# Moving a softmax's reciprocals one beat later and its products two beats later in a fused graph-attention kernel

## The chip, the cores and the metric

The kernel runs on one core of a Trainium2 chip. The time is that of one execution on the device, in microseconds; the median of several runs counts.

## The reference, cut to what matters

Two layers over x of 8 x 2048 x 256 (float32) and a 0/1 adjacency matrix of 2048 x 2048. Layer 0 is an attention of four heads whose softmax runs over each chunk of 256 keys separately; the eight chunks' results are added:

```python
scores = jnp.einsum('bhnd,bhjcd->bhnjc', q, kc) / jnp.sqrt(Dh)
scores = jnp.clip(scores, -10.0, 10.0)
scores = jnp.where(mask == 0, -10.0, scores)
attn = jax.nn.softmax(scores, axis=-1)          # over the 256 keys of one chunk
ctx = jnp.einsum('bhnjc,bhjcd->bhnd', attn, vc)
out = layernorm(ctx @ Wo.T + bo + x) * gamma + beta
h = layernorm(x + out)
```

Layer 1 is a graph attention with one head on h:

```python
Wh = h @ W;  e = leaky_relu(s_i[:, None] + s_j[None, :])    # s_i = Wh @ a1, s_j = Wh @ a2
e = where(adj > 0 or diagonal, e, -inf)
out = layernorm(h + elu(softmax(e) @ Wh))
```

## The kernel before, in words

The kernel writes the order of every engine's work out by hand. For each of 8 batches (b) and 4 blocks of 512 queries (ib) it walks over 8 chunks (j) of 256 keys, J counting all 256 chunks. A chunk takes two **beats** of 128 keys each (`half` 0 and 1, here even and odd), so that there are 512 beats with attention (`2 * total`), and then beats of the tail that hold only layer 1 and the ends of blocks.

In one beat `begin_beat` starts steps of layer 1; then PE computes the scores of the beat (`sc`, line 775, into one of only two PSUM buffers of pool `ps_s`), DVE clips and masks them in place (line 785), ACT exponentiates them (`e`, line 788), and `middle_of_beat` masks layer 1's weights. Then PE multiplies the exponentials of the chunk before (`prev`) with the values and with ones (line 801): in the even beat part 2, the sums over the keys, and part 0, half of the values; in the odd beat part 1, the other half. ACT copies the values' products into `un` and the sums into `ds`. `end_beat` follows.

A chunk's softmax is divided only behind the product with the values. The sums go by a DMA into a narrow tile `dc` of 128 x 16, DVE takes the reciprocals (`inverse`, line 823), a DMA stores them to DRAM (`rd`), another loads them back spread over the partitions (`r`, function `spread`), and `scaled` multiplies `un` by `r` on DVE (line 836, or 834 for the first chunk) and adds the product into `ctxT` on POOL (line 837). These three functions are put on an agenda by the beat at which they are to be issued: `inverse` and `spread` for the end of the same beat, `scaled` for two beats later, so that in an even beat the product of the chunk before stands ahead of the reciprocals of this one.

`end_beat` issues in this order: layer 1's matmuls for the steps whose weights are ready (`product`), one step of every generator in `ahead` and `fins`, and then the agenda. The generators are

- `prelude`, which prepares layer 1 of a batch: Wh, and for every row the largest neighbour (`half_max`, line 412, on DVE, with loads `fb` on the SP queue), once all four blocks of the batch have left layer 0 (`fin_near`). `last_prelude` does so for the last batch in the tail.
- `fin`, the end of a layer-0 block: load x, add biases on POOL, wait, the output projection `po` of ctxT (line 331), two normalisations, h to DRAM, the transpose of h.
- `fin1`, the end of a layer-1 block: load `hr` (h) from DRAM, divide, `ex` = exp(hx - 1) on ACT, minimum and maximum on DVE (line 572), add `hr` on POOL (line 573), normalise, store the output.

A layer-1 step takes 128 keys: `low` on ACT, `leaky` on DVE (line 615), `edges` on DVE (line 620), the exponential on ACT, an addition into `acc` on POOL, and the matmuls `us` on PE (line 643, or 658 for the last batch). Up to 1.5 steps a beat are started, 1.1 while the last batch is in layer 0, and 1 in the tail. Every DMA is issued by the one SP queue, in the order of the program; an entry that waits holds up all behind it.

## Time and profile before

| | |
|---|---|
| median of 3 runs | 4439.85 us (4435.65 to 4445.19) |
| profiled execution | 4440.12 us, span of its instructions 4438.3 us |
| mean granted clock of TensorE | 0.975 |
| first and last score matmul of the attention | 36.7 and 4133 us |
| busy: PE, DVE, ACT, POOL | 92%, 77%, 59%, 40% |
| bytes moved | 432.93 MB, mean 98 GB/s |

Times in the profile are microseconds from the span's start, taken in one execution. PE is TensorE's matmuls, PEld its weight loads, DVE VectorE, ACT ScalarE, POOL GpSimd, SP the engine that issues the DMAs. `out<-in` names what an instruction writes and reads, `L785` the line of the kernel. A row of the waits reads: who waited, for whom, us in total, times, the longest. A row of the stages reads: from:to, length, busy us of PE, PEld, DVE, ACT and POOL with their instructions, granted clock, share of DMA time, GB/s. A row of the timeline reads: start, length, engine, line, operation, operands, how many, and in brackets the engine's idle time ahead of it with what ended it.

### The profile page before, as it was taken

To read this page: it belongs to the slowest core of one execution; us is meant where nothing else is said; L and a number is where in the kernel's file an instruction comes from. 1 tells how busy PE (TensorE), PEld (TensorE's weight loads), DVE (VectorE), ACT (ScalarE), POOL (GpSimd) and SP (SyncE) were. 2 spreads that over 40 slices of the span, in tenths; PEclk is the share of its full clock that TensorE was granted. 3 is DMA by queue.
4 is the path that set the end of the run, shared out by engine and by line. 5 is a ranking of instruction groups with operands and counts; after the bars stand their busy time and mean duration, and the time that the engine had idled before them with its cause. 6 is when DMAs were issued, how large, how long until landed. Compare 5 with 4: busy or idle time off the path is not lost. (4 is left out here: it accounts for less than half of the span.)

```text
span 4438.3 us, 61328 instructions
## 1 busy us (share of the span) xinstructions
PE 4076.7 (92%) x23053; PEld 1913.9 (43%) x23053; DVE 3412.6 (77%) x4530; ACT 2604.1 (59%) x3878; POOL 1782.7 (40%) x906
## 2 busy tenths in 40 slices
PE   7888999999899999999989999999989999899767
PEld 3222334444344443445434453444534445344455
DVE  4776468985799758996599966898569975898786
ACT  4666456665556655666556655566555665566455
POOL 0222224553255523554334543455325543355521
PEclk9999999999999999999999999999999999999889
DMA  4555333322322323223333223332332232332321
GB/s 145 165 161 154 93 104 102 96 89 82 102 84 90 100 67 113 86 79 95 93 92 101 82 75 106 97 105 74 90 105 83 92 96 75 109 94 78 117 79 53
DMA packets 266601, 432.93 MB, mean 98 GB/s; under 512 B 85952, under 2 KB 121024, under 8 KB 265408
## 3 DMA queue, kind: packets, MB, share of 16 engines
q1 hardware_dynamic: 266304, 429.01, 31.5%
q8 instruction: 181, 2.97, 0.3%
q14 instruction: 116, 0.95, 0.1%
HBM read 357.96 MB, written 68.88 MB: 96 GB/s over the span
## 5 line engine op out<-in xcount | busy, mean ns | idle before, releaser
L788 ACT ACTIVATE e<-sc 128x1024 f32<-128x1024 f32 x1024 | 1037.3, 1022 | 1144.9 <-DVE sc L785 1100.5
L785 DVE SCALAR_TENSOR_TENSOR sc<-sc,mk 128x1024 f32<-128x1024 f32 x1024 | 1205.5, 1221 | 519.6 <-PE sc L775 287.1
L775 PE MATMUL sc<-qT,kT 64*128 64x512 f32 x4096 | 1063.6, 633 | 108.6 <-ACT e L788 105.9
L837 POOL TENSOR_TENSOR ctxT<-ctxT,un 128x1024 f32<-128x1024 f32 x224 | 564.9, 2522 | 1173.6 <-DVE un L836 1068.1
L801 PE MATMUL u<-e,v 128*32 128x512 f32 x8192 | 982.5, 597 | 0.0
L643 PE MATMUL us<-wh,w 128*128 128x256 f32 x3584 | 875.9, 393 | 74.3 <-ACT w L624 56.6
L643 PEld LDWEIGHTS us<-wh,w 128*128 128x128 f32 x3584 | 663.9, 192 | 416.6 <-ACT w L624 110.6
L633 POOL TENSOR_TENSOR acc<-acc,w 128x512 f32<-128x512 f32 x392 | 607.8, 1551 | 528.6 <-ACT w L624 512.7
L775 PEld LDWEIGHTS sc<-qT,kT 64*128 64x128 f32 x4096 | 347.5, 189 | 631.3 <-ACT e L788 310.8
L615 DVE SCALAR_TENSOR_TENSOR w<-ab,sj,w 128x512 f32<-128x512 f32 x512 | 587.6, 1168 | 15.4 <-ACT w L611 15.3
L801 PEld LDWEIGHTS u<-e,v 128*32 128x32 f32 x8192 | 240.3, 110 | 660.2 <-issue 539.6
L620 DVE TENSOR_TENSOR w<-w,mk 128x512 f32<-128x512 f32 x512 | 467.8, 934 | 42.9 <-DMA mk<-mask 40.0
L801 PE MATMUL u<-e,ones 128*32 128x512 f32 x4096 | 497.8, 604 | 0.0
L412 DVE CUSTOM_DVE_ANT_0 fb<-sj_row,fb 128x1024 bf16<-128x1024 f32 x240 | 383.8, 1608 | 2.4 <-DMA fb<-far 2.4
L611 ACT ACTIVATE w<-ab,sj 128x512 f32<-128x512 f32 x512 | 353.7, 716 | 18.0 <-PE us L658 11.9
L624 ACT ACTIVATE w<-w 128x512 f32<-128x512 f32 x512 | 310.5, 631 | 66.3 <-DVE w L620 64.9
L836 DVE TENSOR_TENSOR un<-un,r 128x1024 f32<-128x1024 f32 x224 | 278.8, 1244 | 88.2 <-DMA r<-rd 72.7
L809 ACT COPY un<-u 128x512 f32<-128x512 f32 x512 | 300.6, 587 | 54.8 <-PE u L801 52.9
L801 PEld LDWEIGHTS u<-e,ones 128*32 128x32 f32 x4096 | 107.7, 110 | 357.3 <-issue 315.7
L823 DVE RECIPROCAL dc<-dc 128x16 f32<-128x16 f32 x256 | 64.1, 250 | 180.3 <-DMA dc<-ds 155.2
L573 POOL TENSOR_TENSOR hx<-hx,hr 128x1024 f32<-128x1024 f32 x32 | 91.6, 2862 | 177.8 <-DVE hx L572 177.8
L658 PE MATMUL us<-wh,w 128*128 128x257 f32 x512 | 127.6, 412 | 28.8 <-ACT w L624 28.8
(100 smaller groups left out, 3163.1 us busy)
## 6 DMA issues: line engine op xcount, KB each, us to landing
r<-rd SPq DMA_DIRECT2D x256, 256.0 KB
mk<-mask SPq DMA_DIRECT2D x120, 512.0 KB
fb<-far SPq DMA_DIRECT2D x240, 256.0 KB
xT_k<-in_xT_dram SPq DMA_DIRECT2D x32, 512.0 KB
raw<-in_adjT_dram SPq DMA_DIRECT2D x32, 512.0 KB
xT_q<-in_xT_dram SPq DMA_DIRECT2D x32, 512.0 KB
rawf<-in_adj_dram SPq DMA_DIRECT2D x32, 512.0 KB
xT_v<-in_xT_dram SPq DMA_DIRECT2D x32, 512.0 KB
```

Of the source, the lines that this page charges most:

```text
L412: nc.vector.tensor_tensor_reduce(out=fb, in0=sj_row[:, ts(hf, HN)], in1=fb, scale=1.0, scalar=2 * FAR * 0.999, op0=ALU.add, op1=ALU.max, a ...
L611: nc.scalar.activation(self.w, k["ab"][:, 1, :], AF.Identity, bias=k["sj"][:, 1, c : c + 1])
L615: nc.vector.scalar_tensor_tensor(self.w, k["ab"][:, 0, :], k["sj"][:, 0, c : c + 1], self.w, ALU.add, ALU.max)
L620: nc.vector.tensor_tensor(self.w, self.w, self.k["mks"][self.c // HT][:, self.c % HT, :], ALU.min)
L624: nc.scalar.activation(self.w, self.w, AF.Exp)
L633: nc.gpsimd.tensor_add(k["acc"], k["acc"], self.w)
L643: nc.tensor.matmul(k["us"][:, t, :], self.w[:, ts(t, P)], k["wh"][:, c, 0:F], start=(first and t % 2 == 0), stop=last, skip_group_check=True,)
L775: nc.tensor.matmul(sc[:, h, :], kT[h * D : (h + 1) * D, hp, ts(c, P)], qT[h * D : (h + 1) * D, hp, :], start=True, stop=True,)
L785: nc.vector.scalar_tensor_tensor(scs[hp], scs[hp], -CLIP, cap, ALU.max, ALU.min)
L788: nc.scalar.activation(e, scs[hp], AF.Exp)
L801: nc.tensor.matmul(m[h * DH : (h + 1) * DH, :], prev["v"][:, pc, f0 : f0 + DH] if part < 2 else ones[:, 0:DH], prev["es"][2 * i + h // 2][ ...
L837: nc.gpsimd.tensor_add(p["ctxT"], p["ctxT"], p["un"])
```

## The change

- The agenda is issued at the start of `end_beat`, ahead of layer 1's matmuls and of the generators.
- While attention runs, `inverse` and `spread` are issued one beat later, and `scaled` two beats later (`lag`); for the last chunk they keep their beats.
- `fin` no longer counts beats: it waits until the product of the block's last chunk has been issued (`ctx_done`), and while attention runs until the beat behind that.
- `un` gets a third buffer. The space comes from `ds` (one buffer for two) and from `ex`, which now takes turns with `hr` in one buffer; the load of `hr` is therefore issued behind the minimum and maximum that read `ex`, and `fin1` has one beat more before the addition. The second half of `a_bc`, which had `ex`'s place at the start, has that of `y`.

```diff
-        t = one.tile([P, F], F32, tag=("hx", "ex")[n], name=f"a_bc{n}")
+        t = one.tile([P, F], F32, tag=("hx", "y")[n], name=f"a_bc{n}")
...
+    ctx_done = {}
...
         nc.gpsimd.tensor_add(xt, xt, bc_rows(beta_bc))
-        yield
-        yield
-        yield
+        while (b, ib) not in ctx_done or ctx_done[b, ib] == beat < 2 * total:
+            yield
...
     def fin1(b, ib, hx, acc):
-        hr = one.tile([P, TPB, F], F32, tag="hr", name=f"hr{b}_{ib}")
-        nc.sync.dma_start(out=hr, in_=h_d[b, ib])
         yield
...
-        ex = one.tile([P, TPB, F], F32, tag="ex", name=f"ex{b}_{ib}")
+        ex = one.tile([P, TPB, F], F32, tag="hr", name=f"ex{b}_{ib}")
         nc.scalar.activation(ex, hx, AF.Exp, bias=shifts[:, 2:3])
         yield
         nc.vector.scalar_tensor_tensor(hx, ex, 1.0, hx, ALU.min, ALU.max)
+        hr = one.tile([P, TPB, F], F32, tag="hr", name=f"hr{b}_{ib}")
+        nc.sync.dma_start(out=hr, in_=h_d[b, ib])
+        yield
         nc.gpsimd.tensor_add(hx, hx, hr)
...
     def end_beat():
         nonlocal weighted
+        for fn in agenda.pop(beat, []):
+            fn()
         for s in weighted:
             s.product()
         weighted = []
         for gens in (ahead, fins) if beat < 2 * total else (fins, ahead):
             for g in list(gens):
                 if next(g, g) is g:
                     gens.remove(g)
-        for fn in agenda.pop(beat, []):
-            fn()
...
-                    prev["un"] = two.tile([P, 2, IB], F32, tag="un", name=f"un{prev['name']}")
+                    prev["un"] = three.tile([P, 2, IB], F32, tag="un", name=f"un{prev['name']}")
...
-                        ds = two.tile([P, IB], F32, tag="ds", name=f"ds{prev['name']}")
+                        ds = one.tile([P, IB], F32, tag="ds", name=f"ds{prev['name']}")
...
+                            if p["j"] == NCH - 1:
+                                ctx_done[p["b"], p["ib"]] = beat
                             if p["j"] == NCH - 3:
                                 fins.append(fin(p["b"], p["ib"], p["ctxT"]))
-                        at(beat, inverse)
-                        at(beat, spread)
-                        at(beat + 2, scaled)
+                        lag = 1 if J < total else 0
+                        at(beat + lag, inverse)
+                        at(beat + lag, spread)
+                        at(beat + 2 + 2 * lag, scaled)
```

More of the change, by code (lines that the diff above doesn't have):

```diff
@@ L308, in bc_rows @@
         return v.unsqueeze(1).to_broadcast([P, TPB, F])
+    total = B * NIB * NCH
     h_d = dram.tile([B, NIB, P, TPB, F], F32, name="h_d")
@@ L584, in tile_adj_attention__then__gat @@
     states = [{"ab": {}} for _ in range(B)]
-    total = B * NIB * NCH
     def layer1():
```

## The prediction

> **What bounds the kernel now.** I read the page first, then the waits of PE, then busy time by stage, then the timeline around the moved instructions. The page's first part and four of its groups (after the bar: busy us and mean ns; then the idle time of that engine just ahead, and what ended it):
>
> ```profile
> PE 4076.7 (92%) x23053; PEld 1913.9 (43%) x23053; DVE 3412.6 (77%) x4530; ACT 2604.1 (59%) x3878; POOL 1782.7 (40%) x906
> ...
> L837 POOL TENSOR_TENSOR ctxT<-ctxT,un 128x1024 f32<-128x1024 f32 x224 | 564.9, 2522 | 1173.6 <-DVE un L836 1068.1
> ...
> L412 DVE CUSTOM_DVE_ANT_0 fb<-sj_row,fb 128x1024 bf16<-128x1024 f32 x240 | 383.8, 1608 | 2.4 <-DMA fb<-far 2.4
> ...
> L836 DVE TENSOR_TENSOR un<-un,r 128x1024 f32<-128x1024 f32 x224 | 278.8, 1244 | 88.2 <-DMA r<-rd 72.7
> ...
> L823 DVE RECIPROCAL dc<-dc 128x16 f32<-128x16 f32 x256 | 64.1, 250 | 180.3 <-DMA dc<-ds 155.2
> ```
>
> PE sets the time. The change can remove no PE work, only PE's idle time, and it aims at two DVE waits: 180 us ahead of the reciprocals and 88 us ahead of the products. Those 268 us are idle time of an engine that is 77% busy, so they are not yet time of the kernel. By stage (head with the masks, steady loop, tail without attention):
>
> ```profile
> 36.70:494.60 457.90, 383.21 (x2204) 127.97 (x2204) 301.54 (x422) 268.62 (x335) 106.44 (x46) 0.93 0.48 149
> 494.60:4141.50 3646.90, 3468.94 (x19991) 1615.29 (x19991) 2883.34 (x3736) 2175.15 (x3270) 1596.93 (x814) 0.99 0.30 91
> 4141.50:4438.30 296.80, 202.10 (x820) 161.54 (x818) 224.42 (x361) 148.77 (x260) 78.57 (x41) 0.86 0.24 81
> ```
>
> The first number after the comma is PE: 75 us idle in the first stretch, 178 in the second, 95 in the tail, which the change hardly touches. So what can be won lies in 253 us. PE's waits in those first two stretches:
>
> ```profile
> PE sc L775 <- ACT e L788: 105.9, 72, 6.9
> PE po L331 <- POOL ctxT L837: 23.3, 15, 5.1
> PE pq L252 <- ACT un L809: 23.0, 14, 4.6
> PE us L643 <- ACT w L624: 22.3, 33, 2.5
> ```
>
> The largest is the score matmul that waits for the exponential freeing its PSUM buffer: the exponential waits for the clip, and the clip for DVE. One place, in order of time:
>
> ```profile
> 1197.74 0.56 SPq L817 DMA_DIRECT2D dc<-ds  x1
> ...
> 1197.89 1.23 DVE L836 TENSOR_TENSOR un<-un,r 128x1024 f32<-128x1024 f32 x1 [1.23 <-DMA r<-rd]
> ...
> 1201.38 0.25 DVE L823 RECIPROCAL dc<-dc 128x16 f32<-128x16 f32 x1 [2.27 <-DMA dc<-ds]
> 1201.55 2.33 DVE L785 SCALAR_TENSOR_TENSOR sc<-sc,mk 128x1024 f32<-128x1024 f32 x2
> ...
> 1202.79 2.15 ACT L788 ACTIVATE e<-sc 128x1024 f32<-128x1024 f32 x2 [1.97 <-DVE sc L785]
> ...
> 1203.87 2.26 PE L775 MATMUL sc<-qT,kT 64*128 64x512 f32 x8 [1.18 <-ACT e L788]
> ```
>
> DVE is idle 2.27 us until the 8 KB of sums land, the clips behind it start that much late, and 1.18 us of it reach PE. A beat's slack eats the rest.
>
> **How much of the waits reaches PE.** I followed each of PE's waits of the two stretches back by releasers: the exponential, its clip, then DVE's unbroken run of work back to where DVE was last idle. Of 254 us, 99 lead to a wait for dc (63 at score matmuls, 20 at pq, 10 at pw, 6 elsewhere), 12 to a wait for r, 64 to y<-po (DVE waiting for the output projection), 18 to a mask load, and 61 to other places. Where PE's wait is longer than the cause, only the cause can go: the lesser of the two, summed over dc and r, is 94 us.
>
> **Part by part.** A beat of the first half ("even") issues both u products and the copy into ds; the other is "odd".
>
> *Reciprocals.* The reciprocal goes from the end of an even beat to the odd beat behind, after its clips. The 0.56 us issue and the landing (together 3.6 us in the excerpt, from 1197.74 to 1201.38) then have a beat of 7.4 us on average to hide in (the spacing of the score matmuls of even beats): at nothing, and if that cover failed it is the 99 us again. The 0.25 us instruction itself now delays the clips of the following even beat. By the slack (from the end of the exponential that frees a buffer to the score matmul that takes it), 0.25 us later in every such beat costs PE 6 us in all. The store of rd and the load of r move with it on SP. SP's own row has 394 us of waiting for the reciprocal and 409 us for rd to land; these now stand in the odd beat, ahead of the fb loads and the mask loads of the next beat. Mask loads end 40 us of DVE idleness now, 18 of them at PE; moving it to the other parity I take as zero, with 10 us either way.
>
> *Products.* Two beats later, three beats behind the load of r: the 12 us go, they are in the 94. The product now stands ahead of the generators' DVE work, not behind it. [...]
>
> ```profile
> 1215.97 0.66 DVE L615 SCALAR_TENSOR_TENSOR w<-ab,sj,w 128x512 f32<-128x512 f32 x1
> 1216.03 2.80 POOL L837 TENSOR_TENSOR ctxT<-ctxT,un 128x1024 f32<-128x1024 f32 x1 [14.40 <-DVE un L836]
> ...
> 1219.41 2.31 DVE L412 CUSTOM_DVE_ANT_0 fb<-sj_row,fb 128x1024 bf16<-128x1024 f32 x1
> ...
> 1221.65 1.76 DVE L615 SCALAR_TENSOR_TENSOR w<-ab,sj,w 128x512 f32<-128x512 f32 x1
> ```
>
> The first DVE instruction behind the product slips ahead of POOL (0.66 us, and POOL takes 2.80 instead of 2.37); one that meets a running addition loses 1.1 us (L412 2.31 instead of 1.21, L615 1.76 instead of 0.66). In 98 of the 255 even beats with a product, a half_max (L412) stands ahead of it now. After the change half_max slips ahead of POOL and the leaky (L615) behind it is caught: 1.1 us, where it loses 0.5 on average today, so 0.6 more. Slack decides again: in 30 of those beats there is none and in 50 less than 1.1 us, so 0.6 us later costs 18 us in sum, 1.1 us costs 35. Bounds 0 and 35; I take 18.
>
> [...] The rows show a step of 1.1 us, less than half an addition, so the sum goes by the rows.
>
> In the 65 even beats whose generators issue normalisations instead, statistics that POOL does not slow (L292 stays at 400 ns in all its groups) come between product and leaky: nothing lost. In the 92 with no generator work, dc waits are most frequent (71 beats, 111 us), and the leaky behind such a wait falls into the addition; without the wait it slips ahead. I count no extra gain.
>
> *Output projection.* It starts two beats later, again one beat behind the last product, which is now issued earlier in its beat; of its 23 us of waiting for ctxT, 15 are already in the 99 and the 12; I take 5 of the rest.
>
> *Layer 1 a beat or two later.* The states reach the next layer two beats later. For seven batches a stretch with no layer-1 step absorbs it (beats of 7.0 us in one block of each batch). For the last but one, about two steps at 2.0 us of PE move out of the loop into the tail, where a beat with one step takes 2.4 to 4.7 us (L643 in 4230 to 4258): +1 to +5, I take 3. In the tail the last output projection comes one beat sooner: -5 to 0, not counted.
>
> *hr.* Its load now stands behind the minimum/maximum that reads ex, and SP waits for that. Inside the loop a beat covers it. At the very end nothing does: the addition waits for 512 KB. The nearest row is the last store, of equal size: issued at 4434.38, over at 4438.3, so +3.9 us.
>
> *Third un buffer, single ds, ex in hr's place, a_bc in y's:* no instruction and no wait that I find; a product is three beats behind its copies.
>
> Sum: -94 - 5 + 6 + 18 + 3 + 4 = -68 us on the profiled execution's 4440.1 (span 4438.3; the median of the runs, 4439.9, is the same within 0.3 us). Forecast 4372 us.
>
> **Rivals.**
> 1. *The addition takes back what the wait gave* (slower). If every even beat with generator work lost a whole addition, 2.37 us, ahead of the next clips, the slack prices it at 107 us in the half_max beats and 104 in the other 65: -94 + 211 + 6 + 3 + 4 = +130, so 4570 us. It decides from about 1.3 us a beat (46 + 50 us). For it: clips follow on DVE's work without idling in 155 of those 163 beats. Against: no row shows more than 1.1 us lost at one meeting, and statistics do not collide.
> 2. *Next in line* (no change). Behind the removed wait something else is as late, chiefly the leaky or ACT's copies: two thirds of the 94 stay, -31 + 31 = 4440. For it: the other 143 us of PE's waits have other roots. Against: the excerpt, where nothing but the landing stands ahead of the clips.
> 3. *More than the lesser:* the whole 111 us go since the leaky is no longer caught behind a wait, and half_max costs nothing: 4440 - 111 - 10 + 6 = 4325.
>
> **How the numbers follow.** About 0.2% (9 us) is what a measurement of this kernel can tell from no change. Forecast and its surroundings (4331 to 4431) 0.69; rival 3 0.10; rival 2 0.08; rival 1 0.13. Faster: the first two, 0.79; same 0.07, from rival 2; slower 0.14, rival 1 with a bit of 2. The range: 4315 (rival 3 with the mask's 10 us) to 4440 (rival 2, the whole no-change case) leaves out rival 1 and a little.
>
> **What would show it.** In the changed profile: the idle time ahead of the reciprocal (180 us) near zero and that ahead of L836 under 15; PE's waits at sc for the exponential from 106 to about 50, and at pq and pw for ACT's un (36) to under 10; L412's mean up from 1608 ns or L615's up from 1168 where the collision is; the last addition of hx waiting for its DMA. Wrong if the two waits go and PE's idle time stays: then look at L615 and L412; or if a new idle time before w L620 for the mask, or before hx for hr, is over 20 us.

## The result and the profile after

The changed kernel takes 4461.4 us (median of four runs, 4458.1 to 4466.5) beside 4439.1 us for the kernel before (four runs on the same chip). The ratio is 1.005, with a 95% interval of 1.0035 to 1.0064: 22 us or 0.5% slower, where 4372 us was forecast. The profiled execution took 4463.8 us (span 4462.0, mean granted clock 0.967; before 4440.1, 4438.3 and 0.975), so its spans differ by 23.7 us, and the readings below are made against that difference.

The lines of the page and of its groups that answer to those shown of before:

```profile
PE 4091.8 (92%) x23053; PEld 1924.4 (43%) x23053; DVE 3444.0 (77%) x4530; ACT 2603.3 (58%) x3878; POOL 1773.3 (40%) x906
...
L838 POOL TENSOR_TENSOR ctxT<-ctxT,un 128x1024 f32<-128x1024 f32 x224 | 627.7, 2802 | 1376.8 <-DVE un L837 1200.1
...
L616 DVE SCALAR_TENSOR_TENSOR w<-ab,sj,w 128x512 f32<-128x512 f32 x512 | 642.2, 1274 | 20.5 <-ACT w L612 20.3
...
L413 DVE CUSTOM_DVE_ANT_0 fb<-sj_row,fb 128x1024 bf16<-128x1024 f32 x240 | 332.3, 1393 | 23.9 <-DMA fb<-far 23.9
...
L837 DVE TENSOR_TENSOR un<-un,r 128x1024 f32<-128x1024 f32 x224 | 287.2, 1282 | 0.0
...
L824 DVE RECIPROCAL dc<-dc 128x16 f32<-128x16 f32 x256 | 61.7, 241 | 53.4 <-DMA dc<-ds 34.3 <-issue 19.1
```

The change did what it says. The idle time ahead of the products is gone (88.2 to 0.0 us), and that ahead of the reciprocals fell from 180.3 to 53.4 us. The idle time of half_max for its load fb rose from 2.4 to 23.9 us. In the collisions with POOL, leaky (L616) got slower, 1168 to 1274 ns, and half_max (L413) faster, 1608 to 1393 ns. PE is busy 15 us longer with the same instructions. Its waits:

```profile
PE sc L776 <- ACT e L789: 96.3, 54, 6.7
PE us L644 <- ACT w L625: 58.5, 32, 8.3
PE pab L436 <- ACT ds L816: 50.4, 27, 3.4
...
PE po L332 <- POOL ctxT L838: 9.3, 1, 9.3
```

(Over the whole execution the kernel before has 56.6, 16.7 and 23.3 us in the last three of these; the rows of before in the prediction leave out the tail.) PE's wait for the exponential only fell from 105.9 to 96.3 us, and PE's idle time between the first and the last score matmul from 252.6 to 242.1 us: most waits of DVE went, most waits of PE stayed. By stretches (first batch, the rest of the loop, all behind the last score matmul):

```profile
35.80:471.90 436.10, 377.33 (x2206) 123.89 (x2206) 342.57 (x421) 271.33 (x335) 100.78 (x43) 0.95 0.49 155
471.90:4125.00 3653.10, 3469.71 (x19916) 1618.01 (x19915) 2868.73 (x3726) 2163.71 (x3258) 1587.47 (x811) 0.98 0.29 90
4125.00:4462.00 337.00, 222.28 (x898) 173.43 (x894) 229.35 (x373) 156.72 (x272) 84.36 (x47) 0.84 0.23 75
```

From here on "the loop" is the stretch from the first to the last score matmul, and "the tail" all that follows. The loop took 4096.2 us before and 4089.1 us now, the tail 305.4 and 337.0 us, and the start 0.9 us less. So -7.1 + 31.6 - 0.9 = +23.6 us, and the loop holds two layer-1 steps fewer (422 instead of 424). In the loop the first batch, which has no layer 1 yet, gains 22 us, and the steady batches together give 15 back (before, they take 3638.3 us, from 494.6 to the last score matmul at 4132.9; the row in the prediction runs on to 4141.5). Two questions follow: why does the loop keep only 7 us, and why is the tail 32 us longer?

### The profile page after: what moved, and what is told of

The parts are those of the page before. It is cut to its first block, busy times and chain, and to the rows that moved or that the text cites. A ratio compares the mean times of both kernels' runs of the same rounds, so it can differ in the third digit from the quotient of the medians.

```text
span 4462.0 us, 61159 instructions
## 1 busy us (share of the span) xinstructions
PE 4091.8 (92%) x23053; PEld 1924.4 (43%) x23053; DVE 3444.0 (77%) x4530; ACT 2603.3 (58%) x3878; POOL 1773.3 (40%) x906
## 5 line engine op out<-in xcount | busy, mean ns | idle before, releaser
L838 POOL TENSOR_TENSOR ctxT<-ctxT,un 128x1024 f32<-128x1024 f32 x224 | 627.7, 2802 | 1376.8 <-DVE un L837 1200.1
L776 PE MATMUL sc<-qT,kT 64*128 64x512 f32 x4096 | 1075.1, 642 | 100.1 <-ACT e L789 96.3
L634 POOL TENSOR_TENSOR acc<-acc,w 128x512 f32<-128x512 f32 x392 | 569.2, 1452 | 618.1 <-ACT w L625 608.5
L616 DVE SCALAR_TENSOR_TENSOR w<-ab,sj,w 128x512 f32<-128x512 f32 x512 | 642.2, 1274 | 20.5 <-ACT w L612 20.3
L621 DVE TENSOR_TENSOR w<-w,mk 128x512 f32<-128x512 f32 x512 | 403.6, 808 | 3.0
L413 DVE CUSTOM_DVE_ANT_0 fb<-sj_row,fb 128x1024 bf16<-128x1024 f32 x240 | 332.3, 1393 | 23.9 <-DMA fb<-far 23.9
L625 ACT ACTIVATE w<-w 128x512 f32<-128x512 f32 x512 | 309.6, 630 | 45.6 <-DVE w L621 42.7
L837 DVE TENSOR_TENSOR un<-un,r 128x1024 f32<-128x1024 f32 x224 | 287.2, 1282 | 0.0
L332 PE MATMUL po<-WT_o,ctxT 128*128 128x256 f32 x512 | 127.3, 401 | 28.1 <-ACT un L810 18.8
L296 POOL TENSOR_TENSOR rstd_a<-rstd_a,nhalf 128x4 f32<-128x4 f32 x32 | 39.1, 1223 | 284.9 <-DVE rstd_a L295 284.9
```

What stands on the lines that cost most here:

```text
L413: nc.vector.tensor_tensor_reduce(out=fb, in0=sj_row[:, ts(hf, HN)], in1=fb, scale=1.0, scalar=2 * FAR * 0.999, op0=ALU.add, op1=ALU.max, a ...
L616: nc.vector.scalar_tensor_tensor(self.w, k["ab"][:, 0, :], k["sj"][:, 0, c : c + 1], self.w, ALU.add, ALU.max)
L621: nc.vector.tensor_tensor(self.w, self.w, self.k["mks"][self.c // HT][:, self.c % HT, :], ALU.min)
L625: nc.scalar.activation(self.w, self.w, AF.Exp)
L634: nc.gpsimd.tensor_add(k["acc"], k["acc"], self.w)
L776: nc.tensor.matmul(sc[:, h, :], kT[h * D : (h + 1) * D, hp, ts(c, P)], qT[h * D : (h + 1) * D, hp, :], start=True, stop=True,)
```

## The experiments

Loop lengths are those of one profiled execution each. Ratios are to the kernel before on the same chip, with the 95% interval. The medians of the kernel before were 4430 to 4439 us in the groups of runs, so two loop lengths that lie less than some 9 us apart tell nothing by themselves. Where ratio and loop length differ, both are given.

### What the two waits are worth

The kernel before, with the arithmetic kept but the waits taken away: the reciprocal takes the sums of the chunk before and the product the r of the chunk before.

```diff
-                            nc.vector.reciprocal(p["dc"], p["dc"])
+                            p["di"] = two.tile([P, IB // DH], F32, tag="di", name=f"di{p['name']}")
+                            nc.vector.reciprocal(p["di"], last.get("dc", p["dc"]))
+                            last["dc"] = p["dc"]
...
-                            r2 = p["r"].unsqueeze(1).to_broadcast([P, 2, IB])
+                            r2 = last.get("r", p["r"]).unsqueeze(1).to_broadcast([P, 2, IB])
+                            last["r"] = p["r"]
```

> The kernel before, with nothing moved, but the reciprocal takes the sums of the chunk before and the product takes the reciprocals of the chunk before, so that neither waits for its own transfer; the pairing of sums and values is what it leaves out (dc and r get a third buffer, ds has one). Theory A (the two waits are worth what the prediction said, and the rest of the change takes it back): faster than before by 70 to 110 us, PE's idle time in the loop (253 us) down to 150 to 180. Theory B (behind each removed wait something else is as late): faster by 10 to 40 us, PE's idle time in the loop 215 to 245, the clips idle before the score matmuls instead.

Measured: 4357.4 us beside 4437.7, ratio 0.9824 (0.9808 to 0.9841); the loop takes 4015.7 us, 80.5 less. The prediction's first term, -94, was nearly right. What was wrong must lie in what the change does beside removing the waits.

The same cut in the changed kernel takes away what is left of the wait for dc:

```diff
-                            nc.vector.reciprocal(p["dc"], p["dc"])
+                            p["di"] = two.tile([P, IB // DH], F32, tag="di", name=f"di{p['name']}")
+                            nc.vector.reciprocal(p["di"], last.get("dc", p["dc"]))
+                            last["dc"] = p["dc"]
```

> The changed kernel, but the reciprocal takes the sums of the chunk before, so that it never waits for its own transfer; the pairing of sums and values is what it leaves out. If the 53 us that the reciprocals still wait there (38 us of PE's idle time lead to them) are part of what is missing: 30 to 45 us faster than the changed kernel (4461), in the loop. If something else is as late there: within 10 us of it.

Measured: 4444.0, ratio 1.0030 (1.0018 to 1.0042), loop 4069.8. By the loop lengths what is left of the wait costs 19 us, by the ratios (1.0050 to 1.0030) only 9. Even without either wait the changed kernel's loop is 54 us longer than that of the kernel before without them.

### Single parts of the change in their place

The reciprocal alone one beat later, at the end of the odd beat, the product where it was:

```diff
-                        at(beat, inverse)
-                        at(beat, spread)
+                        lag = 1 if J < total else 0
+                        at(beat + lag, inverse)
+                        at(beat + lag, spread)
```

> The kernel before with one part of the change: reciprocals, store of rd and load of r one beat later; products, order of the beat, buffers and tail as before. Theory A: the 180 us ahead of the reciprocals go and the wait for r grows (it has one beat instead of two): 30 to 70 us faster. Theory B: 0 to 25 us faster. If the transfers now come too late, the idle time ahead of the products rises above 150 us and it is slower than before.

Measured: 4738.2, ratio 1.0674 (1.0658 to 1.0691). The product now waits 487 us (and at first chunks 89 us more) for r, which leaves one beat later. So the reciprocal can't go to the end of the odd beat without a later product.

The changed kernel with the agenda at the end of `end_beat` again, as before the change:

```diff
     def end_beat():
         nonlocal weighted
-        for fn in agenda.pop(beat, []):
-            fn()
...
                 if next(g, g) is g:
                     gens.remove(g)
+        for fn in agenda.pop(beat, []):
+            fn()
```

> The changed kernel, but with the agenda at the end of the beat again: everything one and two beats later, the product behind the generators' work and not in front of it; in the tail the last output projection is then again one beat behind the last products. If the order inside the beat takes the gain back (half_max and leaky behind the addition): 40 us or more faster than the changed kernel, of that 15 to 20 in the tail. If only the tail differs: 15 to 20 us faster than the changed kernel (4441 to 4446 where that has 4461), loop as long as its 4088 us.

Measured: 4459.1, ratio 1.0049 (1.0034 to 1.0064), loop 4089.3. The order is worth nothing here, in either direction, although leaky falls from 1274 to 998 ns and the wait for dc rises from 53 to 87 us.

The changed kernel with the output projection of the tail again one beat behind its last product:

```diff
-        while (b, ib) not in ctx_done or ctx_done[b, ib] == beat < 2 * total:
+        while (b, ib) not in ctx_done or ctx_done[b, ib] == beat:
```

> The changed kernel with one condition different: also in the tail the output projection is issued in the beat behind the last product. If the early projection is what lengthens the tail (PE waits 9.3 us for ctxT in front of the transposes that the last prelude needs): 14 to 20 us faster than the changed kernel, and the first matmul of the last batch about 137 us behind the last score matmul instead of 155 (128 before). If the tail is longer because of the two layer-1 steps moved into it: within 4 us of the changed kernel.

Measured: 4454.3, ratio 1.0039 (1.0026 to 1.0053). The stretch from the last score matmul to the last batch's first `us` falls from 155.2 to 146.6 us (before: 128.3). These 8.6 us are seen in the changed kernel's timeline:

```profile
4146.56 1.99 PE L644 MATMUL us<-wh,w 128*128 128x256 f32 x8 [0.99 <-ACT w L625]
...
4152.13 5.67 POOL L838 TENSOR_TENSOR ctxT<-ctxT,un 128x1024 f32<-128x1024 f32 x2 [2.49 <-DVE un L837]
...
4157.85 6.36 PE L332 MATMUL po<-WT_o,ctxT 128*128 128x256 f32 x16 [9.30 <-POOL ctxT L838]
...
4164.04 0.27 PE L389 MATMUL psj<-ident,sj 128*8 128x128 f32 x1
```

The projection, issued in the same beat as its last product, stands ahead of the transposes psj on PE's queue. PE idles 9.30 us for the last addition, and psj with the chain behind it starts at 4164.0; with the projection a beat later it started at 4147.5, in an execution whose loop ended within 1 us of this one's.

The kernel before with only the part on `fin1` (ex and hr in one buffer, the load of hr behind the minimum and maximum, one more beat):

```diff
         nc.vector.scalar_tensor_tensor(hx, ex, 1.0, hx, ALU.min, ALU.max)
+        hr = one.tile([P, TPB, F], F32, tag="hr", name=f"hr{b}_{ib}")
+        nc.sync.dma_start(out=hr, in_=h_d[b, ib])
+        yield
         nc.gpsimd.tensor_add(hx, hx, hr)
```

> The kernel before with only the change's part in the end of the layer-1 block: ex in hr's buffer, hr loaded behind the minimum and maximum, one beat more ahead of the addition. Theory F: 25 to 50 us slower in the loop and 4 to 5 at the end. Theory P: loop within 8 us of before, 4 to 5 us slower at the end (the load of hr with nothing beside it).

Measured: 4444.0 beside 4430.6, ratio 1.0025 (1.0014 to 1.0036), 6 to 16 us. The loop has the length of the one before within what can be told (4096.8), and what follows the last `us` matmul is 4 us longer; where the rest of the ratio, some 7 us, lies stays open. The 4 us in the changed kernel:

```profile
4444.99 1.23 DVE L571 SCALAR_TENSOR_TENSOR hx<-ex,hx 128x1024 f32<-128x1024 f32 x1 [2.31 <-ACT ex L569]
...
4446.25 0.32 SPq L573 DMA_DIRECT2D hr<-h_d  x1
...
4449.77 2.34 POOL L575 TENSOR_TENSOR hx<-hx,hr 128x1024 f32<-128x1024 f32 x1 [32.34 <-DMA hr<-h_d]
```

From 4446.22, when the minimum/maximum is over, to 4449.77 the load is on the path: 3.6 us.

### Is it when layer 1 starts?

The kernel before with the preparation of layer 1 (`prelude`) two beats later, all else untouched:

```diff
     def prelude(b):
...
+        yield
+        yield
```

> The kernel before with one part of what the change brings along: the preparation of layer 1 starts two beats later in every batch but the last. Theory P (layer 1 two beats later is what the loop loses): loop 25 to 50 us longer, and two steps more in the tail, +8 to +10 there; in sum 30 to 60 us slower than before. Theory F (the end of the layer-1 block, with its own beat and the late hr, is what the loop loses): only the tail, +5 to +10 us, loop within 8 us of before.

Measured: 4553.8, ratio 1.0280 (1.0262 to 1.0297), loop 4199.4, +103 us. Two empty beats in one generator cost more than all of the change. PE's idle time that leads back to DVE waiting for the output projection rises from 64 to 129 us, and that which leads to dc from 99 to 123.

The opposite, in the kernel of the tail experiment: two empty steps taken out of `prelude`, so that layer 1 starts in the beats of before.

> The kernel e4_tail_po (4454 us) with two beats of waiting taken out of the preparation of layer 1, so that layer 1 starts where it does in the kernel before. Theory P: the loop 25 to 50 us shorter than e4_tail_po's 4089 us and the tail's two extra steps gone (8 to 10 us): 4395 to 4420. Theory F: the tail's 8 to 10 us only, 4443 to 4448. If the transfers of hT or of far come too late for the earlier start, the loop is longer by the waits for them.

Measured: 4529.0, ratio 1.0218 (1.0203 to 1.0234), loop 4178.8, 90 us longer than with the late start. Half_max now waits 84 us for fb; one of the two steps taken out stood between the issue of the fb loads and half_max, so the run mixes an earlier start with less time for these loads. So the place of the preparation relative to the output projection matters to both sides, and moving it alone repairs nothing.

The changed kernel (with the tail's projection a beat behind) with the output projection and layer 1 in their old beats; the projection then reads ctxT without the product of the block's last chunk, which is left out:

```diff
-        while (b, ib) not in ctx_done or ctx_done[b, ib] == beat:
-            yield
+        yield
+        yield
+        yield
...
+                        def begun(p=prev):
                             if p["j"] == NCH - 3:
                                 fins.append(fin(p["b"], p["ib"], p["ctxT"]))
...
+                        at(beat + 3, begun)
```

> The kernel e4_tail_po (4454 us) with reciprocals and products late as there, but the end of the layer-0 block in the beats that it had before the change, and so layer 1 too; the output projection then reads ctxT without the last chunk's product, which is what it leaves out (but for the last block). Theory S (the loop's gain of some 80 us is there, and shifting the ends of both layers' blocks by two beats against the attention's own cycle takes 40 to 60 us of it back, and two steps move into the tail): 4375 to 4405. Theory R (the late reciprocals and products themselves cost it, by the SP queue and by late fb loads): 4435 to 4455.

Measured: 4460.7, ratio 1.0063 (1.0048 to 1.0078), loop 4108.6. Undoing the shift of the output projection and layer 1 did not shorten the changed kernel's loop, it lengthened it by 20 us (4088.9 in the tail experiment). So the shift is not the sole cause. The next group suggests why: with the projection in its old beats, the new order alone costs 92 us there. The changed kernel with both the order and these beats undone was not run.

The same base with the last batch's rate of layer-1 steps raised, to bring the two steps that had moved into the tail back into the loop:

```diff
-    RATE, LAST_RATE = 1.5, 1.1
+    RATE, LAST_RATE = 1.5, 1.2
```

> The kernel e4_tail_po (4454 us) with 1.2 in place of 1.1 steps of layer 1 a beat while the last batch is in layer 0: about 3 steps more in the loop, 3 less in the tail. If each step in the tail costs what the comparison with the kernel before says (18 us for two): 10 to 25 us faster than e4_tail_po. If the tail is set by the preparation of the last batch and not by the steps: within 5 us.

Measured: 4446.7, ratio 1.0035 (1.0024 to 1.0046). The loop holds 424 steps again, as before the change, and the stretch to the last batch's first `us` falls from 146.6 to 130.1 us. In the other runs with 424 steps in the loop this stretch takes 127 to 131 us, in those with 422 it takes 140 to 155. So two steps more in the tail go with some 10 to 18 us more there. But the loop grows by 6.7 us, and by the ratios the whole run is only some 2 us faster than the tail experiment, which is no difference that can be told: bringing the steps back gained next to nothing.

### Each part alone, without the waits

With the waits gone, the parts can be put in one at a time. The base is the kernel of the first experiment, with a loop of 4015.7 us. First the reciprocal, the store of rd and the load of r one beat later (the edit of the second group):

> The kernel without the two waits (reciprocals of the sums of the chunk before, products with the r of the chunk before), and in it only the reciprocal, the store of rd and the load of r one beat later; the product, the generators and layer 1 keep their beats. Theory Q (the late store and load stand ahead of the fb and mask loads on SP and hold them up, and this is what takes the gain back): the loop ends some 35 to 55 us later than without the waits (4050 us), at 4085 to 4105, and the time is 4390 to 4415; idle time ahead of L413 rises from about 3 to over 30 us. Theory P (it is the later product, and with it the output projection and layer 1): the loop ends within 15 us of 4050, the time is 4350 to 4375. Theory O (it is the order, the product ahead of the generators): as theory P.

Measured: 4348.4, ratio 0.9814 (0.9799 to 0.9828), loop 4005.9, no longer than without this edit. The idle time for mask loads falls from 43 to 11 us, that for fb rises from 2 to 12. Theory Q falls: the later DMAs alone cost nothing.

Then the new order alone, agenda first (with one empty step more in `fin`, so that its work keeps its beats):

> The kernel without the two waits, and in it only the order of the end of a beat turned round: the reciprocal, its DMAs and the product ahead of layer 1's matmuls and of the generators, in the same beats as before (fin gets one more empty step, so its steps keep their beats). Theory O (the product and its POOL addition ahead of the generators' DVE work take the gain back): loop end 30 to 60 us later, 4080 to 4110, time 4385 to 4420, with idle time of PE behind y<-po over 85 us. Theories Q and P: loop end within 15 us of 4050, time 4350 to 4375.

Measured: 4448.9, ratio 1.0042 (1.0027 to 1.0057), loop 4107.7. The order alone costs 92 us here, the whole gain. One place of it:

```profile
1723.31 1.29 DVE L621 TENSOR_TENSOR w<-w,mk 128x512 f32<-128x512 f32 x2 [5.64 <-DMA mk<-mask]
...
1725.88 3.29 POOL L842 TENSOR_TENSOR ctxT<-ctxT,un 128x1024 f32<-128x1024 f32 x1 [15.50 <-DVE un L841]
...
1726.90 2.82 DVE L616 SCALAR_TENSOR_TENSOR w<-ab,sj,w 128x512 f32<-128x512 f32 x1
...
1729.65 2.35 DVE L787 SCALAR_TENSOR_TENSOR sc<-sc,mk 128x1024 f32<-128x1024 f32 x2
...
1731.98 3.65 PE L777 MATMUL sc<-qT,kT 64*128 64x512 f32 x8 [1.86 <-ACT e L790]
```

The wait for the mask load is in the base as well (42.7 us in sum there, 40.8 here). What is new is behind it: the product now stands ahead of half_max, the POOL addition, with half_max beside it, takes 3.29 us (2.37 is the median in the kernel before), and leaky, caught behind the addition, takes 2.82 us instead of 0.70. The clips are that much later, and the score matmuls take 3.65 us behind 1.86 us of idle time, where those at 1718.67 in the same execution took 1.99. In the whole execution 91 leakys take over 2 us (28 in the base), and their mean rises from 1046 to 1274 ns. Of the roughly 11 us that a batch with layer 1 loses, 7.5 fall into its second block, where half_max runs.

Then the product two beats later, with the output projection and layer 1 behind it, in the old order and with the reciprocals in their old beats:

> The changed kernel with reciprocals of the sums of the chunk before, the reciprocals and their DMAs in their old even beat, the old order of the end of a beat, and r in three buffers: of the change there remain the product two beats later, the output projection and layer 1 behind it two beats later, and the shared buffer of ex and hr. Neither wait is left. Theory P: loop end 4085 to 4110, time 4420 to 4450 (the tail is some 25 us longer as in the changed kernel). Theories Q and O: loop end 4045 to 4070, time 4385 to 4410. If every one of these three runs gives back 15 to 25 us, the loss is a sum of all three parts, and no single one carries it.

Measured: 4438.8, ratio 1.0018 (1.0008 to 1.0028), loop 4071.2, +55.5 (this run and its split below also hold the part on `fin1`), so the third part also takes back most of the gain. The idle time for fb is 47.5 us (2.0 in the base) and that for y behind po 91.4 us (62.8).

This part was split once more. First the product late, the output projection and layer 1 in their old beats:

```diff
-        while (b, ib) not in ctx_done or ctx_done[b, ib] == beat:
-            yield
+        yield
+        yield
+        yield
...
+                        def begun(p=prev):
                             if p["j"] == NCH - 3:
                                 fins.append(fin(p["b"], p["ib"], p["ctxT"]))
...
+                        at(beat + 2, begun)
```

> The run with the late product and no waits, but the output projection and layer 1 back in the beats of the kernel before (the projection then reads ctxT without the last chunk's product; that is left out). Theory A (the product itself, three beats behind its r, is what costs: it meets other work on DVE and POOL): the loop, from first to last score matmul, stays at 4060 to 4085 us as in that run (4072). Theory B (what costs is the output projection, with it the loads of fb and layer 1, two beats later): the loop falls to 4005 to 4030, as without the waits (4016), and idle time ahead of y for po and ahead of fb falls from 87 and 41 to below 65 and 15.

Measured: 4380.1, ratio 0.9886 (0.9872 to 0.9901), loop 4027.9, +12.2. By the ratios it is 28 us more than the base, of which 6 lie in the tail, so 12 to 22 us.

Then the reverse, the product in its old beat and the output projection two beats later (with the part on `fin1` and the buffers that go with it, not shown here):

```diff
         nc.gpsimd.tensor_add(xt, xt, bc_rows(beta_bc))
         yield
+        yield
+        yield
...
-            ctxT = one.tile([P, 2, IB], F32, tag="ctx", name=f"ctxT{b}_{ib}")
+            ctxT = two.tile([P, 2, IB], F32, tag="ctx", name=f"ctxT{b}_{ib}")
```

> The other half: the kernel without the two waits, its products and reciprocals in their old beats, and in it only the output projection two beats later (two more empty steps in fin; ctxT gets a second buffer for it, ex shares the buffer of hr), so that normalisations, fb loads and layer 1 come two beats later too. Theory B: loop 4060 to 4085 us, idle time ahead of y for po over 75. Theory A: loop 4005 to 4030.

Measured: 4407.7, ratio 0.9947 (0.9930 to 0.9963), loop 4054.6, +38.9 (by the ratios 55 us more than the base, of which 18 lie in the tail, so 37). The two halves add up to 51 of the 55.5 us (by the loops), and the larger is the output projection with layer 1 behind it. Theory B was right in kind, and a quarter or more of the loss is theory A's. In this run the places are the same in every batch. At beats 20 and 21 of the batch, in order of time:

```profile
1647.69 1.18 SPq L406 DMA_DIRECT2D fb<-far  x2
...
1653.58 1.23 DVE L414 CUSTOM_DVE_ANT_0 fb<-sj_row,fb 128x1024 bf16<-128x1024 f32 x1 [2.77 <-DMA fb<-far]
...
1661.10 3.36 PE L333 MATMUL po<-WT_o,ctxT 128*128 128x256 f32 x7 [4.28 <-ACT un L813]
```

Half_max waits 2.77 us for its load, the clips behind it are late, and PE waits. By the walk back through the releasers, PE's idle time behind fb is 4.6 us at beat 21 of each of batches 1 to 6 (none in the base), and behind y<-po it is 3.2 us at beat 54 (none in the base, which has some 3.6 us behind y<-po at beat 22 instead). PE's idle time in the loop rises by 22 us in all, from 199 to 221; the rest of the 38.9 us is in its busy time. By blocks of four a batch (means of batches 2 to 6, counted from 0, against the base), the first takes 4.9 us more, with 11 layer-1 steps in place of 8, the second 2.0 us less, with 5 in place of 8, and the fourth 3.6 us more.

### Versions between the two

The kernel before with the reciprocal in the odd beat, but at once behind the clips, ahead of `edges`, and the product in its old beat:

```diff
     def middle_of_beat():
         nonlocal edged
+        while mids:
+            mids.pop(0)()
...
-                        at(beat, inverse)
-                        at(beat, spread)
+                        if J < total:
+                            mids += [inverse, spread]
...
                         at(beat + 2, scaled)
```

> The kernel before with the reciprocals, store and load behind the clips of the odd beat, ahead of the edges, and everything else in its old beat, the product included; no buffer added. Theory S: no phase is shifted, so most of the 80 us stay: 4360 to 4400, the idle time ahead of the reciprocal under 60 us; the wait for r grows from 73 us to at most 150, as its 4 to 5 us fit between the clips of one beat and the end of the next. If r comes too late, as in e2_recip_only (577 us of waiting for it): over 4480.

Measured: 4402.4 beside 4432.1, ratio 0.9937 (0.9921 to 0.9952), loop 4063.3. It beats both kernels by taking the reciprocals' part only: the wait for dc is 3 us, and the wait of the products for r rises to 152 us. The same with the reciprocal at the front of the odd beat's `end_beat`:

> As e10_recip_mid, but reciprocals and their transfers at the front of the end of the odd beat, behind the edges, where the changed kernel has them. Some 1 to 2 us later than e10_recip_mid in each odd beat: if r has the time, equal to it within 15 us; if r is what decides, 30 to 150 us slower than it, and still faster than e2_recip_only (4738), which has them behind the generators' work.

Measured: 4410.3, ratio 0.9947 (0.9930 to 0.9963); the wait for r is 156 us.

The faster of these two with the product one beat later, a third `un`, and ex in hr's place, to remove the wait for r too:

```diff
-                        at(beat + 2, scaled)
+                        at(beat + (3 if J < total else 2), scaled)
```

> The kernel before with the reciprocals behind the clips of the odd beat (as in the run that beat both kernels, 4402), and the product one beat later, at the end of the odd beat, with a third un buffer, a single ds, and ex in hr's place; the output projection and layer 1 keep their beats, which in the old order leaves the output projection directly behind the last product's beat. If the 152 us of idle time ahead of the products cost PE what theory says (a third to a half reaches it): that idle time under 20 us, the loop ends at 4050 to 4070 against 4096, time 4360 to 4385. If the waits are only replaced by others (the output projection for ctxT, fb loads): 4400 to 4430.

Measured: 4470.3, ratio 1.0091 (1.0076 to 1.0106), loop 4115.5. The wait for r is gone, and the loop is 52 us longer than with it: the wait for y behind po is 113 us (67 without the edit), that for dc 99 (3), that for fb 22 (9). Again the removal of a wait on DVE was no gain in itself.

## Why the prediction was wrong, by its steps

**The first term was right.** It said -94 for the waits that reach PE; taking them away gave -80.5 in the loop. The lesser of PE's wait and of its cause was a fair measure.

**The step that failed is "For seven batches a stretch with no layer-1 step absorbs it".** This counted the block's end and layer 1 two beats later at nothing within the loop. Alone, in the kernel without the waits, they cost 38.9 us. There the second block of a batch, where that stretch lies, gave 2.0 us back for three steps less, while the first block of the next batch took 4.9 us more for three steps more. So a shift against the attention was no delay that a slack stretch takes up. The generators' loads and DVE work fall beside other beats, and the same two beats of the batch lose 4.6 and 3.2 us each time. How it happens is seen for fb, in the changed kernel at the start of layer 1's preparation:

```profile
1667.61 0.42 SPq L393 DMA_DIRECT2D sj_d<-sjr  x1
...
1668.44 0.58 ACT L816 COPY ds<-u 128x512 f32<-128x512 f32 x1
...
1672.50 0.33 SPq L394 DMA_DIRECT2D sj_row<-sj_d  x1
...
1672.88 0.90 SPq L405 DMA_DIRECT2D fb<-far  x2
...
1673.88 0.56 SPq L818 DMA_DIRECT2D dc<-ds  x1
...
1678.47 0.25 DVE L824 RECIPROCAL dc<-dc 128x16 f32<-128x16 f32 x1 [5.49 <-issue]
...
1678.75 0.31 SPq L826 DMA_DIRECT2D rd<-dc  x1
...
1680.79 0.90 SPq L405 DMA_DIRECT2D fb<-far  x2
...
1683.25 3.79 PE L776 MATMUL sc<-qT,kT 64*128 64x512 f32 x8 [4.46 <-ACT e L789]
...
1687.07 1.22 DVE L413 CUSTOM_DVE_ANT_0 fb<-sj_row,fb 128x1024 bf16<-128x1024 f32 x1 [2.68 <-DMA fb<-far]
```

**"Have a beat of 7.4 us on average to hide in", for the landing, failed at the same place.** The mean was used, and the beats here are not mean: the odd beat that was to hide it, from the score matmuls at 1669.4 to those at 1673.1, is 3.8 us long. The sums were in ds at 1669.0, but SP stood 4.5 us at the load of sj_row until the store of sj_d that it reads had landed, and the 8 KB were issued only at 1673.88, behind these loads on the same queue (1670 to 1682):

```profile
sj_row<-sj_d SPq DMA_DIRECT2D x1, 1024.0 KB
fb<-far SPq DMA_DIRECT2D x4, 256.0 KB
```

DVE idled 5.49 us at the reciprocal. (This row names no releaser; at the same beat of three other batches the row names dc<-ds, after 3.6 to 4.7 us.) SP stood behind it with the store of rd and the next two fb loads (issued 1680.79), and half_max then waited 2.68 us for these. PE lost 4.46 us, and 1.8 us more since the eight matmuls took 3.79 us instead of 1.99. Over the whole execution SP's wait for the reciprocal rose from 394.0 to 969.4 us. The prediction had named SP's queue and the fb loads, but priced only the mask loads, and those did gain (40 us of waiting before, none now). In all, what is left of the dc wait is the 9 to 19 us in the sum below.

**"Two beats later": the product itself.** The prediction counted its order and the 12 us that go; its new place costs 12 to 22 us.

**The order: the price of one meeting was too low, and in the changed kernel its sum too high.** The prediction read a loss of 1.1 us from two rows; the changed kernel shows leaky at 2.85 us behind an addition of 3.19 us, where one alone takes 0.70:

```profile
1202.28 1.22 DVE L413 CUSTOM_DVE_ANT_0 fb<-sj_row,fb 128x1024 bf16<-128x1024 f32 x1
...
1202.53 3.19 POOL L838 TENSOR_TENSOR ctxT<-ctxT,un 128x1024 f32<-128x1024 f32 x1 [10.27 <-DVE un L837]
...
1203.43 2.85 DVE L616 SCALAR_TENSOR_TENSOR w<-ab,sj,w 128x512 f32<-128x512 f32 x1
```

So leaky loses 2.15 us. Half_max slipped ahead and leaky was caught, as the prediction said. The two rows with 1.1 us were misread: the addition into ctxT shown with them was over at 1218.83, and half_max and leaky met the shorter additions into acc (1.84 and 1.75 us) behind it. The whole loss stood in the kernel before as well, where 61 of the 512 leakys take over 2 us:

```profile
1218.79 1.84 POOL L631 TENSOR_TENSOR acc<-w,w 128x512 f32<-128x512 f32 x1
...
1244.87 2.37 POOL L837 TENSOR_TENSOR ctxT<-ctxT,un 128x1024 f32<-128x1024 f32 x1 [6.37 <-DVE un L836]
1244.97 2.81 DVE L615 SCALAR_TENSOR_TENSOR w<-ab,sj,w 128x512 f32<-128x512 f32 x1
```

So the first rival's "no row shows more than 1.1 us" holds for the rows shown and not for the trace. Alone, in the kernel without the waits, the order costs 92 us, and in the changed kernel nothing (4089.3 against 4088.9). That the second block of a batch runs 5.0 layer-1 steps there instead of 8.0, and so has slack for it, fits but was not tested. At the places of 2.85 and 2.81 us leaky, begun with 2.3 us of the addition still to run, ended 0.5 to 0.6 us behind the addition's end (at 1206.28 behind 1205.72, and in the kernel before at 1247.78 behind 1247.24), so it lost all but 0.2 us of what was left. In the two rows of the prediction 1.2 us of the additions into acc were left, and 1.1 us was lost.

**The tail: +7 counted, +31.6 measured.** The load of hr was right (4 counted, 3.6 on the path at the end, whatever its part in the loop). "+1 to +5" for two steps of layer 1 was wrong: 146.6 - 128.3 = 18.3 us. The prediction priced them by beats with one step each at the end of this stretch; they stand at its start, ahead of the last batch's preparation. Raising the rate took 16.5 us out of the stretch again, though not out of the run. "-5 to 0" for the projection one beat sooner was wrong in sign, +8.6, since the projection, issued sooner, only waits sooner, and the transposes behind it on PE's queue wait with it.

The sum in loop lengths, each from one run:

| | us |
|---|---|
| both waits gone (4096.2 to 4015.7) | -80.5 |
| product two beats later (to 4027.9) | +12.2 |
| output projection and layer 1 two beats later (4015.7 to 4054.6) | +38.9 |
| the rest: order, later reciprocal, interplay (4066.8, the sum so far, to 4069.8) | +3.0 |
| what is left of the dc wait (4069.8 to 4089.1) | +19.3 |
| tail: two steps 18.3, projection 8.6, hr and the rest 4.7 | +31.6 |
| start | -0.9 |
| sum, as measured | +23.6 |

Worked out from the ratios instead, less the difference of the tails, the first five lines are some -78, +21, +37, +2 and +9 us, so that a single line is known to about 10 us. The second and third line were measured in the kernel without the waits, each alone, and together there as +55.5; both hold the part on `fin1`, so that what it costs in the loop may count twice. That the rest is as small as 3 us is no proof that the parts are the same in the changed kernel: this rest holds the order, which alone costs 92 us, and undoing the shift of the third line in the changed kernel won nothing. So the parts do not simply add; a line says what that step cost in this sequence, and not what undoing it alone would bring.

**The rivals.** The one on the slower side had the right sign, but its mechanism, the addition taking the gain back at 4570 us, holds only for the order alone. "Next in line" came nearest with its time of 4440, by luck: its mechanism, that something else is already as late behind each removed wait, is refuted by the first experiment, where 80 of the 94 us went. What stood there in the changed kernel (fb, y<-po) came with the moves. The third rival's sum has a term of -10 that it does not explain; the result lies far from it either way.

**Signs named ahead.** Right: L837's idle time at 0.0, pq and pw for un from 36 to 6 us, L616 slower, the last addition waiting for hr. Wrong: PE's wait at sc (96, not 50) and the reciprocal's (53, not near zero). The sentence "Wrong if the two waits go and PE's idle time stays" held, and so did the one on hr: POOL idles 137.4 us ahead of the additions of hr, in ten places, 32.3 of them at the end. The places to look were not the collisions but fb and y<-po.

Left open: why two beats between preparation and attention make 103 us in the kernel before. The runs show where PE idles (y<-po), not a rule that gives the best shift.

## What to carry to other kernels

A wait's worth and the price of the move that removes it are two numbers: take the wait away by itself first, with stale data, and then add each part of the move alone. Work that follows the moved step by "a beat behind" moves too, and in a kernel whose queues are written out by hand each such shift is priced by the beats that it lands on, the shortest and the most loaded ones, not by the mean beat. Where one queue carries both the small transfer that gates an engine and large loads, look what is issued just ahead of it.

## What the runs showed of the hardware

In this kernel a stall of PE cost more than its length. Around the stall above, the windows read (third number from the end: granted clock):

```profile
1676.00:1678.50 2.50, 2.50 (x28) 0.65 (x20) 0.03 (x1) 0.00 (x0) 0.00 (x0) 1.00 0.71 256
1678.60:1683.20 4.60, 0.19 (x4) 0.00 (x0) 4.60 (x8) 1.02 (x1) 0.00 (x0) 0.84 0.24 61
1683.25:1687.00 3.75, 3.75 (x12) 1.17 (x14) 1.14 (x2) 1.99 (x3) 2.34 (x1) 0.50 0.51 139
1690.00:1700.00 10.00, 8.27 (x52) 4.11 (x54) 9.20 (x20) 2.98 (x4) 1.02 (x1) 1.00 0.45 125
```

Behind the 4.46 us of idle time the granted clock reads 0.50, and the eight score matmuls took 3.79 us, where those at 1669.37, at a granted clock of 1.00, took 1.99. In the tail, the 16 matmuls of po took 6.36 us behind 9.30 us of idle time, at a granted clock of 0.58, and 3.62 us in the kernel before, at 1.00 and with no idle time ahead. The clock's records in these two executions hold only 1.00 and 0.50; they stand at 0.50 for 222 us in the kernel before and 294 us in the changed one (mean granted clock 0.975 and 0.967; without the waits 0.980). Summed over all groups of four or more equal matmuls, the time above the group's median is 12 to 17 us more in the changed kernel than in the kernel before, by how the groups are formed. That is about the 15 us by which PE is busier there with the same instructions, and it is not in its idle time. A shorter stall went with slow matmuls as well: in the place shown of the order alone the score matmuls stood only 1.86 us, and they took 3.65 us. How long a stall must be for this was not measured.
